# Two layers of a convolution and attention network: layer 1's merged, interleaved attention replaced by a plain loop over images, and the experts issued as a software pipeline over units of half an image

## The chip, the cores and the metric

The kernel runs on one core of one Trainium2 chip. The metric is the device time of one execution in microseconds (us); the median of three runs stands for a kernel. All arithmetic is in fp32.

## The reference

The input x has 8 images of 256 channels and 32 x 32 pixels (1024 tokens). Layer 0 is a convolution and attention block that the change does not touch. Layer 1 takes the tokens and computes, for each image:

```
t = t + attn(ln(t));   t = t + experts(ln(t))

attn(E): Q = E WQ^T;  K = E WK^T;  V = E WV^T
         W = Q K^T / 16                       # 1024 x 1024 an image, one head of 256
         e = exp(W - max over the whole row) * (1 where k <= q and W != 0, else 0)
         out = e / (sum e + 1e-9) @ V

experts(x): w = softmax(mean over the images of x @ Wr + br)     # a gate for each token and expert
            h = relu(bn(x W1[e] + b1));  h = relu(bn(h W2[e] + b2));  y = h Wo[e] + bo
            out = sum over the 8 experts of y * w                # every expert sees every token
```

`ln` is a layer norm over the 256 channels without weights. The maximum is over the whole row of W, also over masked places, so all 1024 columns of the logits are computed.

## The kernel before

Channels lie on the partitions in two groups of 128 (`KC`), the tokens of an image along the free dimension, in two halves of 512 (`HALF`). TensorE, VectorE (DVE), ScalarE (ACT), GpSimd (POOL) and SyncE (SP, which issues all DMAs) run side by side. Each fp32 matmul shows in the trace as two passes with a weight load each.

The program has three stages. Layer 0 writes each image to a spill buffer in DRAM, and all eight images are loaded back into `t[0..7]`. Layer 1's attention adds to `t`; `z[b]` is the normed image. The experts read `z` and add to `t`, which is stored.

**Layer 1 (L563 to L730).** At the start `wq` and `wk` are transposed and multiplied into one matrix `mT` (L572 to L591), so that the logits of an image are `(mT z) z^T`. For each image there are four kinds of work. `layer_norm` (L600) is a generator of three pieces: the two channel groups are summed on DVE into `ts` and their mean `mu` is one matmul with a constant matrix; the squares are summed with a thin matrix into `var`, four slices stacked on the partitions, so that the reciprocal runs over 256 elements; `r` is spread again with `sel4` into `rb`. `before1` (L638) norms an image and projects `y` and `v`. `after1` (L663) norms it a second time and adds it to `feat` for the gate. `logits(b, i)` (L670) computes the logits of 128 tokens in `s`, their maximum `nm`, the exponential `pr`, the causal mask on POOL, and the sum; `values(b, i)` (L702) transposes `pr` into `pT`, multiplies by `v` into `po`, scales by the reciprocal sum, transposes back into `tpo` and adds to `t`.

The main loop (L718) writes these in an interleaved order: the logits of tile i, then the values of the tile before, then a share of `before1` of the next image and of `after1` of the previous one.

**Buffers.** A tile pool hands out a fixed number of buffers for each tag. In PSUM `ps_s` has two of 1024 columns (`s`), `ps_t` two for transposes, `ps_m` two of 512 columns under the one tag `mm`: `mu`, `var`, `rb`, `pq`, `pv`, `po` and the gate's `lg` all take from it. In SBUF the tags `pr`, `pT`, `y` and `v` have two buffers each. The order of the instructions of an engine is set when the program is built, from the order written and from what is ready.

**Experts (L760 to L825).** For each expert e the three weight matrices are loaded (two buffers each) and the gate is spread to `wb`. For each image and half, a unit, three layers follow each other: h1 from z (L800, `w1s`), h2 from h1 (L800, `w2s`), then `pye` (L815, `wos`). Each layer is two output groups of two matmuls. ACT applies relu and the batch norm (L804), DVE adds the bias and multiplies by the gate (L819), POOL adds to `t` (L822). The last expert stores each image (L824). The inner order is

```
h1 = ...; layer(h1, w1s, z[b][:, :, hs], s1, o1)
h2 = ...; layer(h2, w2s, h1, s2, o2)
for g in range(KC):  # pye from h2, y, t += y
```

At the very end some tiny instructions (L830 on) check layer 0's sums; a general version of the program (L845 on) stands behind a branch that the inputs don't take.

Of the kernel before, what the change touches and what calls it, by code (L numbers as in the profile page):

```python
# [15 lines left out]
P = 128  # L16
# [62 lines left out]
def fast_body(  # L79
# [465 lines left out]


# [15 lines left out]

    with ExitStack() as l1:  # L563
        wpool = l1.enter_context(tc.tile_pool(name="w1", bufs=1))
        ps_s = l1.enter_context(tc.tile_pool(name="ps_s1", bufs=2, space=PSUM))
        ps_t = l1.enter_context(tc.tile_pool(name="ps_t1", bufs=2, space=PSUM))
        ps_m = l1.enter_context(tc.tile_pool(name="ps_m1", bufs=2, space=PSUM))


        mT = wpool.tile([P, KC, C], F32, name="mT")  # L570
        wv_s = wpool.tile([P, KC, C], F32, name="wv")
        nc.sync.dma_start(wv_s, wvT.rearrange("(k p) o -> p k o", p=P))  # L572
        with tc.tile_pool(name="wset", bufs=1) as wset:
            rows = []
            for nm_, src in (("wq", wqT), ("wk", wkT)):
                w_ = wset.tile([P, KC, C], F32, tag=nm_, name=nm_)
                nc.sync.dma_start(w_, src.rearrange("(k p) o -> p k o", p=P))
                r_ = wset.tile([P, KC, C], F32, tag=f"{nm_}r", name=f"{nm_}r")
                for e in range(KC):
                    tp = ps_t.tile([P, 4, P], F32, tag="tp", name="tpw")  # L580
                    for k in range(KC):
                        nc.tensor.transpose(tp[:, k, :], w_[:, k, e * P : (e + 1) * P], ident)
                    nc.vector.tensor_copy(r_[:, e, :], tp[:, :KC, :])
                rows.append(r_)
            for g in range(KC):
                pm_ = ps_m.tile([P, HALF], F32, tag="mm", name="pmT")
                for e in range(KC):
                    nc.tensor.matmul(
                        pm_[:, :C], rows[0][:, e, g * P : (g + 1) * P], rows[1][:, e, :], start=(e == 0), stop=(e == KC - 1)
                    )  # L590
                nc.scalar.activation(mT[:, g, :], pm_[:, :C], AF.Copy, scale=1.0 / math.sqrt(C))  # L591
        two = l1.enter_context(tc.tile_pool(name="two1", bufs=2))
        feat = wpool.tile([P, KC, N], F32, name="feat")
        sel4 = wpool.tile([P, 4, P], F32, name="sel4")
        nc.gpsimd.memset(sel4, 0.0)
        nc.gpsimd.affine_select(
            out=sel4, in_=sel4, compare_op=ALU.not_equal, fill=1.0, base=0, pattern=[[-32, 4], [0, P]], channel_multiplier=1
        )

        def layer_norm(b):  # L600

            tb, zb = t[b], z[b]
            for h in range(2):
                hs = slice(h * HALF, (h + 1) * HALF)
                ts = two.tile([P, HALF], F32, tag="ts", name="ts", bufs=1)
                nc.vector.tensor_add(ts, tb[:, 0, hs], tb[:, 1, hs])
                mu = ps_m.tile([P, HALF], F32, tag="mm", name="mu")
                nc.tensor.matmul(mu, mean_c, ts, start=True, stop=True)
                nc.vector.tensor_sub(
                    zb[:, :, hs], tb[:, :, hs], mu.rearrange("p (o n) -> p o n", o=1).to_broadcast([P, KC, HALF])  # L610
                )
            yield
            var = ps_m.tile([P, HALF], F32, tag="mm", name="var")
            for k in range(KC):
                sq = two.tile([P, N], F32, tag="sq", name="sq", bufs=1)
                nc.scalar.activation(sq, zb[:, k, :], AF.Square)
                for j in range(4):
                    nc.tensor.matmul(
                        var[32 * j : 32 * j + 32, :QC], mean_c[:, :32], sq[:, j * QC : (j + 1) * QC],
                        start=(k == 0), stop=(k == KC - 1),  # L620
                    )
            r = two.tile([P, QC], F32, tag="r", name="r", bufs=1)
            nc.scalar.activation(r, var[:, :QC], AF.Sqrt, bias=eps_ln)
            nc.vector.reciprocal(r, r)
            yield
            for h in range(2):
                hs = slice(h * HALF, (h + 1) * HALF)
                rb = ps_m.tile([P, HALF], F32, tag="mm", name="rb1")
                for i in range(2):
                    nc.tensor.matmul(rb[:, i * QC : (i + 1) * QC], sel4[:, 2 * h + i, :], r, start=True, stop=True)  # L630
                nc.vector.tensor_mul(
                    zb[:, :, hs], zb[:, :, hs], rb.rearrange("p (o n) -> p o n", o=1).to_broadcast([P, KC, HALF])
                )
            yield

        ys, vs = {}, {}

        def before1(b):  # L638
            yield from layer_norm(b)
            y = two.tile([P, KC, N], F32, tag="y", name="y")  # L640
            for g in range(KC):
                for h in range(2):
                    hs = slice(h * HALF, (h + 1) * HALF)
                    pq = ps_m.tile([P, HALF], F32, tag="mm", name="pq1")
                    for k in range(KC):
                        nc.tensor.matmul(
                            pq, mT[:, k, g * P : (g + 1) * P], z[b][:, k, hs], start=(k == 0), stop=(k == KC - 1)
                        )
                    nc.scalar.copy(y[:, g, hs], pq)
                yield  # L650
            v = two.tile([P, NT, C], F32, tag="v", name="v")
            for j in range(0, NT, 2):
                pv = ps_m.tile([P, 2, C], F32, tag="mm", name="pv")
                for i in range(2):
                    js = slice((j + i) * P, (j + i + 1) * P)
                    for k in range(KC):
                        nc.tensor.matmul(pv[:, i, :], z[b][:, k, js], wv_s[:, k, :], start=(k == 0), stop=(k == KC - 1))
                nc.scalar.copy(v[:, j : j + 2, :], pv)
                if j % 4 == 2:
                    yield  # L660
            ys[b], vs[b] = y, v

        def after1(b):  # L663
            yield from layer_norm(b)
            if b == 0:
                nc.gpsimd.tensor_copy(feat, z[b])
            else:
                nc.gpsimd.tensor_add(feat, feat, z[b])

        def logits(b, i):  # L670

            width = (i + 1) * P
            q0 = i * P
            s = ps_s.tile([P, N], F32, tag="s", name="s1")
            for h in range(2):
                hs = slice(h * HALF, (h + 1) * HALF)
                for k in range(KC):
                    nc.tensor.matmul(s[:, hs], ys[b][:, k, q0 : q0 + P], z[b][:, k, hs], start=(k == 0), stop=(k == KC - 1))  # L678

            nm = small.tile([P, 1], F32, tag="nm", name="nm1")  # L680
            nc.vector.tensor_reduce(nm, s, AX.X, ALU.max, negate=True)
            pr = two.tile([P, N], F32, tag="pr", name="pr1")
            nc.scalar.activation(pr[:, :width], s[:, :width], AF.Exp, bias=nm)
            nc.gpsimd.affine_select(
                out=pr[:, q0:width],
                in_=pr[:, q0:width],
                compare_op=ALU.is_ge,
                fill=0.0,
                base=0,
                pattern=[[-1, P]],  # L690
                channel_multiplier=1,
            )
            sm = small.tile([P, 1], F32, tag="sm", name="sm1")
            nc.vector.scalar_tensor_tensor(
                pr[:, :width], s[:, :width], 0.0, pr[:, :width], ALU.not_equal, ALU.mult, accum_out=sm
            )
            rs = small.tile([P, 1], F32, tag="rs", name="rs1")
            nc.vector.tensor_scalar_add(rs, sm, A_EPS)
            nc.vector.reciprocal(rs, rs)
            return pr, rs  # L700

        def values(b, i, pr, rs):  # L702

            pT = two.tile([P, NT, P], F32, tag="pT", name="pT1")
            transpose_rows(pr, (i + 1) * P, pT, 0, ps_t)
            po = ps_m.tile([P, HALF], F32, tag="mm", name="po1")
            for j in range(i + 1):
                nc.tensor.matmul(po[:, :C], pT[:, j, :], vs[b][:, j, :], start=(j == 0), stop=(j == i))
            ot = two.tile([P, C], F32, tag="ot", name="ot")
            nc.scalar.activation(ot, po[:, :C], AF.Copy, scale=rs)  # L710
# [9 lines left out]
        for b in range(B):  # L720
            prev = Stream(after1(b - 1), AFTER_PIECES) if b else None
            nxt = Stream(before1(b + 1), BEFORE_PIECES) if b + 1 < B else None
            for i in range(NT):
                cur = (b, i) + logits(b, i)
                if late is not None:
                    values(*late)
# [790 lines left out]
```

## Time and profile before

| what | us |
|---|---|
| median of three runs (3762.32 to 3765.38) | 3764.66 |
| the profiled execution | 3762.32 |
| its span | 3760.6 |
| layer 0 ends, all images in the spill buffer, about | 1679 |
| first norm of layer 1 starts (L606) | 1709.5 |
| last norm of layer 1 ends (L631) | 2318.2 |
| first expert matmul (L800) | 2343.8 |
| last store issued (L824) | 3752.8 |

| engine | busy us | share |
|---|---|---|
| PE (matmuls) | 3521.5 | 94% |
| PEld (weight loads) | 1599.2 | 43% |
| DVE | 1632.4 | 43% |
| ACT | 1412.6 | 38% |
| POOL | 389.3 | 10% |

PE is TensorE's matmuls and PEld its weight loads, which run beside them. The busy time of PE is modelled at the end of each matmul, so a short wait between two matmuls doesn't show in it; the starts of the weight loads show it. A line of the timeline gives start and duration in us, engine, line of the program, operation, tiles (output `<-` inputs), shape, count, and in brackets the idle time before it with what ended it. Durations of single instructions in the lists of groups are in ns.

### The profile page before, as it was taken

The page shows a single profiled execution, that of the slowest core. Times are in us where ns is not written, and L with a number is a line of the kernel's source. Part 1 is how long each engine was busy: PE and PEld are TensorE (multiplying, and loading weights), DVE is VectorE, ACT ScalarE, POOL GpSimd, SP SyncE. Part 2 cuts the span into 40 slices and gives each one's busy share as a digit, 9 for nine tenths or more (in the row PEclk, how much of TensorE's full clock was granted, in tenths as well). Part 3 has the DMA queues.
Part 4 walks back from the last instruction along what each step waited for, and adds up shares of the span by engine and source line. Part 5 has one row for each costly group of instructions (what it writes and reads, how often), then busy time and mean ns, then how long its engine had stood idle before and what let it go on. Part 6 is the DMA issues. An engine that isn't in the chain of part 4 may idle for free. (4 is left out here: it accounts for less than half of the span.)

```text
span 3760.6 us, 25274 instructions
## 1 busy us (share of the span) xinstructions
PE 3521.5 (94%) x9924; PEld 1599.2 (43%) x9924; DVE 1632.4 (43%) x1902; ACT 1412.6 (38%) x1850; POOL 389.3 (10%) x357
## 2 busy tenths in 40 slices
PE   7999999999999999737999997999999999999998
PEld 4334444343434343324655664444444444444443
DVE  3368585959595858653454443111111111111111
ACT  4354545455454544202344333222323222222222
POOL 1000000000000000000000101222222222222222
PEclk9999999999999999868999997999999999999999
DMA  1000000000000000011000000000000000000001
GB/s 63 0 0 0 23 0 23 1 23 0 23 0 23 0 12 0 12 64 45 1 1 1 1 1 17 0 9 0 9 1 9 0 9 0 9 0 9 0 34 57
DMA packets 16277, 45.05 MB, mean 12 GB/s; under 512 B 1350, under 2 KB 9494, under 8 KB 14102
## 3 DMA queue, kind: packets, MB, share of 16 engines
q1 hardware_dynamic: 16150, 43.36, 3.1%
q8 instruction: 80, 1.31, 0.1%
q14 instruction: 47, 0.39, 0.0%
HBM read 26.57 MB, written 16.78 MB: 12 GB/s over the span
## 5 line engine op out<-in xcount | busy, mean ns | idle before, releaser
L804 ACT ACTIVATE h<-pm,bn_o,bn_s 128x512 f32<-128x512 f32 x512 | 398.0, 777 | 967.1 <-PE pm L800 967.1
L819 DVE SCALAR_TENSOR_TENSOR y<-pye,vec,wb 128x512 f32<-128x512 f32 x256 | 192.1, 750 | 1219.3 <-PE pye L815 1218.0
L464 DVE SCALAR_TENSOR_TENSOR conv<-hpad,vec,conv 128x1024 f32<-128x1024 f32 x512 | 648.5, 1279 | 9.4
L397 PE MATMUL acc<-p,vT 128*128 128x512 f32 x1024 | 508.7, 629 | 62.9 <-ACT p L395 62.6
L800 PE MATMUL pm<-h,w2s 128*128 128x512 f32 x1024 | 494.5, 605 | 1.4
L815 PE MATMUL pye<-h,wos 128*128 128x512 f32 x1024 | 494.5, 605 | 1.4
L800 PE MATMUL pm<-z,w1s 128*128 128x512 f32 x1024 | 463.3, 595 | 0.0
L822 POOL TENSOR_TENSOR t<-t,y 128x512 f32<-128x512 f32 x256 | 323.6, 1264 | 1105.6 <-DVE y L819 1105.6
L397 PEld LDWEIGHTS acc<-p,vT 128*128 128x128 f32 x1024 | 192.2, 197 | 339.7 <-issue 173.1
L395 ACT ACTIVATE p<-s 128x1024 f32<-128x1024 f32 x256 | 254.9, 1021 | 216.3 <-PE s L393 215.4
L393 PE MATMUL s<-qk 32*128 32x512 f32 x1024 | 316.0, 632 | 0.0
L800 PEld LDWEIGHTS pm<-h,w2s 128*128 128x128 f32 x1024 | 184.0, 189 | 291.1 <-issue 153.6
L815 PEld LDWEIGHTS pye<-h,wos 128*128 128x128 f32 x1024 | 184.0, 189 | 291.1 <-issue 183.7
L800 PEld LDWEIGHTS pm<-z,w1s 128*128 128x128 f32 x1024 | 194.7, 191 | 249.2 <-issue 196.8
L330 PE MATMUL ph<-xn,piw 128*128 128x512 f32 x512 | 246.1, 613 | 18.0 <-ACT hpad L452 18.0
L678 PE MATMUL s<-z,y 128*128 128x512 f32 x512 | 247.2, 596 | 0.0
L393 PEld LDWEIGHTS s<-qk 32*128 32x128 f32 x1024 | 93.0, 184 | 180.3 <-issue 165.5
L560 POOL MEMSET ones<- 1x128 f32 x1 | 0.2, 194 | 1632.2 <-DVE conv L464 1632.2
L330 PEld LDWEIGHTS ph<-xn,piw 128*128 128x128 f32 x512 | 95.4, 194 | 157.3 <-issue 128.9
L480 PE MATMUL pz<-pow__122,hid 128*128 128x256 f32 x512 | 121.9, 389 | 42.9 <-DVE hid L473 42.9
L377 DVE SCALAR_TENSOR_TENSOR o<-vpad,pe_w,o 128x1024 f32<-128x1024 f32 x128 | 161.7, 1275 | 0.3
L452 ACT ACTIVATE hpad<-ph,pi_o 128x512 f32<-128x512 f32 x128 | 87.7, 688 | 173.6 <-PE ph L330 166.6
(190 smaller groups left out, 2943.6 us busy)
## 6 DMA issues: line engine op xcount, KB each, us to landing
t<-in_x_dram SPq DMA_DIRECT2D x8, 1024.0 KB, 5.0
sp<-t SPq DMA_DIRECT2D x8, 1024.0 KB, 3.9
t<-sp SPq DMA_DIRECT2D x8, 1024.0 KB, 9.9
out_dram<-t SPq DMA_DIRECT2D x8, 1024.0 KB, 4.0
w1s<-in_w_dram SPq DMA_DIRECT2D x8, 256.0 KB, 2.7
w2s<-in_w_dram SPq DMA_DIRECT2D x8, 256.0 KB, 2.8
wos<-in_wo_dram SPq DMA_DIRECT2D x8, 256.0 KB, 2.7
piw<-in_pi_wT_dram SPq DMA_DIRECT2D x1, 1024.0 KB, 8.7
```

The lines of the kernel that those rows point to most:

```text
L330: nc.tensor.matmul(ps, w[:, k, o0 : o0 + P], src[:, k, hs], start=(k == 0), stop=(k == KC - 1))
L377: nc.vector.scalar_tensor_tensor(d3, src, wk, d3, ALU.mult, ALU.add)
L393: nc.tensor.matmul(s[:, i, :], qk[kp, 1, m * P : (m + 1) * P], qk[kp, 0, cs], start=True, stop=True)
L395: nc.scalar.activation(p, s, AF.Exp)
L397: nc.tensor.matmul(acc[i], vT[:, m, g, i : i + 2, :], p[:, i, :], start=(m == 0), stop=(m == NT - 1))
L464: nc.vector.scalar_tensor_tensor(d3, src, wk, d3, ALU.mult, ALU.add)
L678: nc.tensor.matmul(s[:, hs], ys[b][:, k, q0 : q0 + P], z[b][:, k, hs], start=(k == 0), stop=(k == KC - 1))
L800: nc.tensor.matmul(pm, w_[:, k, g * P : (g + 1) * P], src[:, k, :], start=(k == 0), stop=(k == KC - 1))
L804: nc.scalar.activation(dst[:, g, :], pm, AF.Relu, bias=bi[:, c : c + 1], scale=sc[:, c : c + 1])
L815: nc.tensor.matmul(py, wos[:, k, g * P : (g + 1) * P], h2[:, k, :], start=(k == 0), stop=(k == KC - 1))
L819: nc.vector.scalar_tensor_tensor(y, py, col("bo", KC * e + g), wb[:, hs], ALU.add, ALU.mult)
L822: nc.gpsimd.tensor_add(t[b][:, g, hs], t[b][:, g, hs], y)
```

## The change

Layer 1 goes to a plain loop over the images. The merged matrix, `ts`, the thin `var`, `sel4` and the generators go. `wq`, `wk` and `wv` are used as loaded. One image after the other is normed, projected, attended and normed again. The norm takes the mean with two matmuls over t and sums the squares with two matmuls over 512 columns, so that `r` and its reciprocal are 128 x 512. The squares are taken on POOL. Queries go in blocks of 256 (`QC`): two tiles of logits, with `pr` scaled by the reciprocal sum on POOL ahead of the transposes, then one `po` with the channels on the partitions, which is added to `t` directly. The pool `one1` gives one buffer each to `sq`, `r`, `q`, `k`, `v` and `pT`.

In the experts a list of units is kept, and step n issues h1 of unit n, h2 of unit n - 1 and `pye` of unit n - 2; `h1` and `h2` have three buffers. Two more steps at the end finish the last units.

```diff
+    def layer_norm(b, work, ps_m):
+        for h in range(2):
+            hs = slice(h * HALF, (h + 1) * HALF)
+            mu = ps_m.tile([P, HALF], F32, tag="mm", name="mu")
+            for k in range(KC):
+                nc.tensor.matmul(mu, mean_c, t[b][:, k, hs], start=(k == 0), stop=(k == KC - 1))
+            sq = work.tile([P, KC, HALF], F32, tag="sq", name="sq")
+            for k in range(KC):
+                nc.vector.tensor_sub(z[b][:, k, hs], t[b][:, k, hs], mu)
+                nc.gpsimd.tensor_mul(sq[:, k, :], z[b][:, k, hs], z[b][:, k, hs])
+            var = ps_m.tile([P, HALF], F32, tag="mm", name="var")
+            for k in range(KC):
+                nc.tensor.matmul(var, mean_c, sq[:, k, :], start=(k == 0), stop=(k == KC - 1))
+            r = work.tile([P, HALF], F32, tag="r", name="r")
+            nc.scalar.activation(r, var, AF.Sqrt, bias=eps_ln)
+            nc.vector.reciprocal(r, r)
+            for k in range(KC):
+                nc.vector.tensor_mul(z[b][:, k, hs], z[b][:, k, hs], r)
...
+        one = l1.enter_context(tc.tile_pool(name="one1", bufs=1))
...
-        mT = wpool.tile([P, KC, C], F32, name="mT")
...
+        def causal_attention(b):
+            layer_norm(b, one, ps_m)
+            q = one.tile([P, KC, N], F32, tag="q", name="q")
+            kk = one.tile([P, KC, N], F32, tag="k", name="kk")
+            for g in range(KC):
+                for h in range(2):
...
+                    for w_, dst, sc in ((wq_s, q, 1.0 / math.sqrt(C)), (wk_s, kk, 1.0)):
+                        pq = ps_m.tile([P, HALF], F32, tag="mm", name="pq1")
...
+                        nc.scalar.activation(dst[:, g, hs], pq, AF.Copy, scale=sc)
+            v = one.tile([P, NT, C], F32, tag="v", name="v")
...
+                nc.vector.tensor_copy(v[:, j : j + 2, :], pv)
+            for qc in range(N // QC):
+                nq = QC // P
+                pT = one.tile([P, NT, QC], F32, tag="pT", name="pT1")
+                for qt in range(nq):
...
+                    s = ps_s.tile([P, N], F32, tag="s", name="s1")
...
+                    nc.vector.tensor_reduce(nm, s, AX.X, ALU.max, negate=True)
+                    pr = two.tile([P, N], F32, tag="pr", name="pr1")
+                    nc.scalar.activation(pr[:, :width], s[:, :width], AF.Exp, bias=nm)
+                    nc.gpsimd.affine_select(out=pr[:, q0:width], in_=pr[:, q0:width],
...
+                    nc.vector.scalar_tensor_tensor(
+                        pr[:, :width], s[:, :width], 0.0, pr[:, :width], ALU.not_equal, ALU.mult, accum_out=sm
+                    )
+                    nc.vector.tensor_scalar_add(rs, sm, A_EPS)
+                    nc.vector.reciprocal(rs, rs)
+                    nc.gpsimd.tensor_scalar(pr[:, :width], pr[:, :width], rs, 1.0, ALU.mult, ALU.mult)
+                    transpose_rows(pr, width, pT, qt * P, ps_t)
+                po = ps_m.tile([P, KC, QC], F32, tag="mm", name="po1")
+                nj = (qc + 1) * nq
+                for g in range(KC):
+                    for j in range(nj):
+                        c0 = max(0, j * P - qc * QC)
+                        nc.tensor.matmul(
+                            po[:, g, c0:], v[:, j, g * P : (g + 1) * P], pT[:, j, c0:], start=(j == 0), stop=(j == nj - 1)
+                        )
+                tb = t[b][:, :, qc * QC : (qc + 1) * QC]
+                nc.vector.tensor_add(tb, tb, po)
+
+        for b in range(B):
+            causal_attention(b)
+            layer_norm(b, one, ps_m)
             if b == 0:
                 nc.gpsimd.tensor_copy(feat, z[b])
             else:
                 nc.gpsimd.tensor_add(feat, feat, z[b])
...
+        def advance(n):
+            if n <= len(units):
+                e, b, h, w1s, w2s, wos, wb = units[n - 1]
+                hidden[n - 1] = layer("h1", w1s, z[b][:, :, h * HALF : (h + 1) * HALF], s1, o1, e)
+            if 0 <= n - 2 < len(units):
+                e, b, h, w1s, w2s, wos, wb = units[n - 2]
+                hidden[n - 2] = layer("h2", w2s, hidden[n - 2], s2, o2, e)
+            if 0 <= n - 3:
+                e, b, h, w1s, w2s, wos, wb = units[n - 3]
+                h2 = hidden.pop(n - 3)
...
+                if e == NE - 1 and h == 1:
+                    nc.sync.dma_start(ov[b], t[b])
...
             for b in range(B):
                 for h in range(2):
+                    units.append((e, b, h, w1s, w2s, wos, wb))
+                    advance(len(units))
+        for i in range(2):
+            advance(len(units) + 1 + i)
```

The new `layer` is the old one with the tile taken inside it and three buffers, and the part of `advance` left out is the old loop over `pye`, `y` and the sum into `t`.

## The prediction

> **What bounds the kernel now.** I read the busy shares first, then the same by stage, then the waits and the order of instructions inside a stage.
>
> ```profile
> PE 3521.5 (94%) x9924; PEld 1599.2 (43%) x9924; DVE 1632.4 (43%) x1902; ACT 1412.6 (38%) x1850; POOL 389.3 (10%) x357
> ```
>
> ```profile
> 1750.00:2300.00 550.00, 548.90 (x2211) 335.98 (x2210) 267.23 (x474) 220.76 (x348) 47.14 (x70) 1.00 0.00 1
> 2300.00:2343.00 43.00, 24.93 (x90) 16.53 (x89) 13.93 (x33) 9.07 (x23) 6.48 (x3) 0.58 0.11 34
> ...
> 2350.00:3750.00 1400.00, 1397.19 (x3092) 564.68 (x3090) 191.34 (x255) 405.10 (x525) 321.30 (x255) 1.00 0.03 9
> ```
>
> The second fence is the table by stretches; its lines give length, busy time of PE, PEld, DVE, ACT, POOL, then the granted clock. TensorE fills both stages that the change touches. In layer 1 (1750 to 2300) it is busy 548.9 of 550 us for eight images: 68.7 us per image, at full clock. In the experts it seems equally full, but ends of matmuls are modelled, so I look at when weights are loaded:
>
> ```profile
> 2905.57 0.19 PEld L800 LDWEIGHTS pm<-z,w1s 128*128 128x128 f32 x1 [0.24 <-DVE y L819]
> ...
> 2909.01 0.19 PEld L800 LDWEIGHTS pm<-h,w2s 128*128 128x128 f32 x1 [0.24 <-ACT h L804]
> ...
> 2910.47 0.30 PEld L800 LDWEIGHTS pm<-h,w2s 128*128 128x128 f32 x2 [0.84 <-ACT h L804]
> ...
> 2912.72 0.19 PEld L815 LDWEIGHTS pye<-h,wos 128*128 128x128 f32 x1 [0.24 <-issue]
> ...
> 2914.18 0.30 PEld L815 LDWEIGHTS pye<-h,wos 128*128 128x128 f32 x2 [0.84 <-ACT h L804]
> ...
> 2916.43 0.19 PEld L800 LDWEIGHTS pm<-z,w1s 128*128 128x128 f32 x1 [0.24 <-DVE y L819]
> ```
>
> Layer w1s, which reads z, takes 3.44 us (2905.57 to 2909.01) for 8 passes (each fp32 matmul is two): 0.43 us a pass. Layers w2s and wos take 3.71: their second k tile waits for the ACT relu of the layer just before. That is 0.27 us lost twice per unit of 10.86 us. Over 128 units the waits list has
>
> ```profile
> PEld pm L800 <- ACT h L804: 137.5, 254, 0.8
> PEld pye L815 <- ACT h L804: 107.4, 128, 0.8
> ```
>
> most of which is the ordinary distance between loads; only 2 x 0.27 us per unit is lost.
>
> One more reading decides what the new layer 1 can overlap. The program is put in order per engine when it is built, not as written: at 52.12 a logits matmul (L393) runs between transposes (L363) that stand before it. But tiles of one pool tag are handed out in the order written:
>
> ```profile
> 9.73 1.04 ACT L306 ACTIVATE xn<-t 128x1024 f32<-128x1024 f32 x1
> ...
> 17.30 3.57 PE L227 MATMUL wv<-vec,qkvw 128*128 128x1 f32 x16
> ...
> 29.33 1.93 PE L310 MATMUL ms<-xn,mean_c 128*32 128x256 f32 x16
> ```
>
> The squares for ms are ready at 10.77 and TensorE is idle until 16.2, yet ms runs at 29.33, after all the wv tiles, its predecessors in tag mm. The same at 1717: image 1's ts is summed at 1716.66, TensorE has gaps until 1727, but mu comes at 1744, in its written place.
>
> [...]at 2343.81 the first expert passes stand 0.85 us apart, from 2348.19 on 0.43; the window 2300 to 2343 has a granted clock of 0.58. [...]layer 1 has 15 of 1283 ns for Sqrt and 15 for Exp in the groups of 1600 to 2300, run ahead of their operand, and the new code needs as many (one to Sqrt, one to Exp an image). For the new POOL scaling of pr no row exists; see below.
>
> **Experts.** The new order puts, between a layer and its reader, at least one other layer of another unit, 3.4 us of TensorE work against a relu of 0.78. ACT (4 x 0.78 us), DVE (2 x 0.75) and POOL (2 x 1.26) have room in 10.3 us, h1 and h2 get a third buffer. On SP, a weight buffer comes free two units later (21 us) for the loads of the expert after next, which have 174 us; the store of an image is issued at its second half, two units after it was, again with 21 us of other units behind it. So 2 x 0.27 x 128 = 69, say **70 us gained**; bounds 0 (a new wait) and 75. The last image's store (3752.8 to the span's end) stays uncovered as it is.
>
> **Layer 1, TensorE work per image.** Two norms of 8 matmuls: 16 x 0.86 = 13.8 (before: ones over ts, thin var, rb). q and k: 16 x 0.86 = 13.8 (merged matrix: 6.9). v: 32 passes of 256 columns at 0.21 = 6.9. Logits 32 x 0.86 = 27.5. Transposes 36 x 0.11 = 3.9 (the ot ones go). po: 32 x 0.43 + 8 x 0.22 = 15.5. Sum 81 against 68.7. Costed at nothing: the q and k copies (8 of 0.59 on ACT in place of 4) and the v copies, now on DVE (4 of 0.69), each under 1.72 us of its next matmuls; ot's scaling, gone from ACT; the sums into t, 4 in place of 8. That is the floor; the order now leaves holes, since norms, projections and po share tag mm, and q, k, v, pT, sq, r have one buffer. So image b+1's norm can't enter before b's second norm, and b's second norm not before its last po. Per image:
>
> Norm pair, from the end of the last po. First half: mu 1.7, subtract 0.69, squares on POOL 2 x 1.26 (row L822), var after them, Sqrt 0.69 (row L452, same form), reciprocal 3.35 (row L414, 128x512), two multiplies of 0.69 (row L422): with hand-overs 13 us. Each further half must wait for r, then Sqrt, reciprocal, multiplies: 0.7 + 3.35 + 1.4 = 5.5, plus 0.7 for a subtract in between, plus the squares, which wait for sq. I get 8.8 for the second, 6.2 for the third, and 7.6 for the fourth, where the feat sum (4.5 us, row L668) sits ahead of the squares on POOL. **36 us**; bounds 30 (reciprocal chain alone) and 42 (half clock, squares slowed).
>
> Projections: the first q and k group hides in the norm; 6 x 1.72 + 6.9 = 17.2, plus 2 for a cold start: **19**; bounds 17 and 23.
>
> Attention: after the last pass of logits i come max 1.22, Exp 0.38 to 1.13, mask 0.29, product 0.29 to 1.22, sum and reciprocal 0.4, POOL scaling, then transposes. The scaling I take at 0.2 + 0.9 ns an element, 0.3 to 1.1 us, from the POOL COPY of 2048 elements (1889 ns)[...]. With two s buffers, logits i+1 and i+2 cover this chain, so TensorE is full for six tiles. By priority the third po (4.7) goes ahead of the end of the eighth logits: these end 40 us after the start. Then nothing covers the last chain: 6 us, transposes and copy 1.3, po 6.5, of which a part at half clock, +2: **55 us**; bounds 49 and 65.
>
> Sum 36 + 19 + 55 = 110 us per image against 68.7.
>
> **Front and end.** The norm of image 0 needs only t[0], the first of eight 1 MB loads issued from 1679 on; at 437 GB/s it lands near 1682. Now wq and wk are transposed and multiplied first (1703 to 1709.8) and the norm starts at 1709.5. So 27 us are won there. Its 22 us end near 1704, when the projection weights, last in the queue, have landed (wk at 1703 now). New end of the last norm: 1682 + 22 + 8 x 74 + 7 x 36 + 22 = 2570, against 2318 now (last multiply 2316.93 + 1.22). **+252 us.** Gate and expert set-up after it are unchanged.
>
> **Sum.** +252 - 70 = +182 on the profiled execution of 3762.3 (span 3760.6 and 1.7 around it). The median of the three runs is 3764.7, so 3947; I say 3945.
>
> **Rivals.** *Overlap after all* (the other side): if the builder does let image b+1's norm run in b's attention, layer 1 is bound by TensorE at 81 us an image. The end is 1690 + 8 p for p us an image (110 gives 2570), so 81 gives 2338: +20 - 70 = -50, 3715. It is faster from p below 87 (1690 + 8 x 87 = 2388). For it: logits are moved ahead. Against: ms and mu above never were. 0.10, of which 0.02 within 0.2% of no change. *Serial tiles*: if transposes i stay ahead of logits i+1, each tile pays 3.4 plus the whole chain: 8 x 3.4 + 8 x 4.9 + 4 + 15.5 + 3 = 89 us, p = 144, end 2842: +524 - 70, 4219[...]. Against: the move at 52.12. 0.10. *Expert gain missing* (a wait on another buffer replaces it): 4017. 0.05. My forecast: 0.75.
>
> **Range.** p from 96 to 130 gives -112 and +160 about 3945. I take 3840 to 4100, which takes in the missing expert gain and leaves out the overlap and the serial case: 0.2. Differences below 0.2% (7.5 us) can't be told from none by a measurement of this kernel. Faster 0.08, within 0.2% 0.02, slower 0.90.
>
> **What would show it.** Expert units of 10.3 us with relu waits gone; last norm's multiply near 2570; 36 us a pair between images with TensorE mostly idle and a clock near 0.5; before each image's last transposes an idle 6 us. Wrong: mu of image b+1 inside attention b (first rival), or 9 us and more from logits to logits (second).

## The result, and the profile after

| kernel | median us | lowest to highest | ratio to before, 95% interval |
|---|---|---|---|
| before, in the same session | 3763.49 | 3759.99 to 3765.38 | |
| after | 3958.36 | 3955.81 to 3959.01 | 1.0518 (1.0499 to 1.0536) |

The change costs 195 us. The profiled execution after took 3958.95 us, its span is 3957.2, 196.6 more than before; all that follows is read against that. From the profile's page, the busy times of the kernel after:

```profile
PE 3600.7 (91%) x9780; PEld 1652.5 (42%) x9780; DVE 1734.9 (44%) x1946; ACT 1349.2 (34%) x1754; POOL 512.1 (13%) x483
```

and its table by stretches (length, busy time of PE, PEld, DVE, ACT, POOL, granted clock, DMA share, GB/s), for layer 1, the end of layer 1 and the experts:

```profile
1702.00:2535.00 833.00, 691.38 (x2054) 364.34 (x2054) 361.26 (x508) 158.89 (x255) 156.78 (x184) 0.90 0.00 1
2535.00:2600.00 65.00, 45.26 (x173) 30.09 (x172) 27.80 (x45) 13.32 (x25) 17.27 (x16) 0.80 0.00 0
2600.00:3940.00 1340.00, 1338.32 (x3114) 591.64 (x3115) 192.42 (x266) 408.54 (x536) 319.25 (x252) 0.99 0.03 10
```

The experts still look full; layer 1 no longer does. TensorE had hardly a gap there before (1.1 of 550 us); now it is idle for 142 of 833 us, and its clock is granted only 0.90. Yet 691 busy us, in a layer that took 609 in all (1709.5 to 2318.2), also mean more work, or slower work. The rest of this section separates these.

**Experts.** The timeline of weight loads after, at the start of each layer of one unit (start, duration, then in brackets the idle time and what ended it):

```profile
2998.37 0.19 PEld L724 LDWEIGHTS pm<-z,w1s 128*128 128x128 f32 x1 [0.24 <-DVE y L749]
...
3001.80 0.19 PEld L724 LDWEIGHTS pm<-h,w2s 128*128 128x128 f32 x1 [0.24 <-ACT h L728]
...
3005.24 0.19 PEld L745 LDWEIGHTS pye<-h,wos 128*128 128x128 f32 x1 [0.24 <-issue]
...
3008.67 0.19 PEld L724 LDWEIGHTS pm<-z,w1s 128*128 128x128 f32 x1 [0.24 <-DVE y L749]
```

All three layers now take 3.43 to 3.44 us, the unit 10.30 in place of 10.86, and the wait of 0.84 us on the relu is gone. From the first expert matmul (2611.4) to the last output's y (3946.9) are 1335.5 us, against 1406.8 before (2343.8 to 3750.6): 71 us won.

**Layer 1.** The first expert matmul comes at 2611.4 in place of 2343.8: 267.6 us lost. 267.6 - 71.3 is 196.3, the whole difference. The stretches of one steady image, from the end of the last `po` of the image before: the pair of norms, the projections, the attention:

```profile
2113.90:2160.20 46.30, 28.79 (x44) 9.58 (x43) 26.22 (x21) 3.94 (x6) 13.85 (x9) 0.71 0.00 1
2160.20:2177.20 17.00, 17.00 (x57) 10.64 (x56) 2.07 (x3) 3.58 (x6) 0.00 (x0) 1.00 0.00 0
2177.20:2226.80 49.60, 47.58 (x179) 28.85 (x179) 20.61 (x44) 13.75 (x22) 8.30 (x16) 1.00 0.00 0
```

This image takes 112.9 us, the mean of the last six is 112.6. For before the same table, from one sum of features to the next:

```profile
2022.30:2094.80 72.50, 72.50 (x293) 44.22 (x293) 35.73 (x63) 29.58 (x46) 6.81 (x9) 1.00 0.00 1
```

So a steady image took 72.5 us, not the 68.7 that I had got by dividing 550 us by eight: that stretch holds some 7.6 images. The forecast's sum did not use the figure, since it counts from the first norm to the last, but the comparison of floors did. TensorE is now idle 17.5 us in the pair and 2.0 in the attention, together 19.5. It is busy 93.4; at full clock its work would be about 81.4 (the prediction's sum, unrounded). So, as an estimate, some 12 us of its busy time are lost to half-clock passes, and 8.9 us (81.4 - 72.5) are added work. 19.5 + 12 + 8.9 = 40.4, which is 112.9 - 72.5. The largest part is idle time, the next half clock, and added work the least.

### The profile page after: what moved, and what is told of

It reads as the page before. It is cut to its first block, busy times and chain, and to the rows that moved or that the text cites. A ratio compares the mean times of both kernels' runs of the same rounds, so it can differ in the third digit from the quotient of the medians.

```text
span 3957.2 us, 25092 instructions
## 1 busy us (share of the span) xinstructions
PE 3600.7 (91%) x9780; PEld 1652.5 (42%) x9780; DVE 1734.9 (44%) x1946; ACT 1349.2 (34%) x1754; POOL 512.1 (13%) x483
## 3 DMA queue, kind: packets, MB, share of 16 engines
q8 instruction: 79, 1.29, 0.1%
## 4 chain that ended last, share of the span: by engine, by line
PE 71%; DVE 19%; ACT 4%; issue 2%; POOL 2%; DMA 1%; ACTq 0%; SPq 0%; DVEq 0%; POOLq 0%
PE pm L724 22%; PE pye L745 11%; DVE conv L464 9%; PE acc L397 7%; PE s L393 3%; PE ph L330 3%; PE s L630 3%; PE po L661 3%; DVE o L377 3%; PE pq L607 3%; PE pz L480 3%; PE pq L330 2%; PE var L574 2%; DVE r L577 1%; PE pv L617 1%
## 5 line engine op out<-in xcount | busy, mean ns | idle before, releaser
L724 PE MATMUL pm<-h,w2s 128*128 128x512 f32 x1024 | 460.3, 592 | 0.0
L745 PE MATMUL pye<-h,wos 128*128 128x512 f32 x1024 | 460.2, 592 | 0.0
L750 POOL TENSOR_TENSOR t<-t,y 128x512 f32<-128x512 f32 x256 | 324.3, 1267 | 1031.3 <-DVE y L749 1031.3
L724 PEld LDWEIGHTS pm<-h,w2s 128*128 128x128 f32 x1024 | 194.6, 190 | 244.9 <-issue 213.6
L745 PEld LDWEIGHTS pye<-h,wos 128*128 128x128 f32 x1024 | 194.6, 190 | 244.9 <-issue 244.9
L630 PE MATMUL s<-kk,q 128*128 128x512 f32 x512 | 236.4, 597 | 10.4 <-DVE pr L648 5.6
L574 PE MATMUL var<-sq,mean_c 128*128 128x512 f32 x128 | 107.6, 946 | 123.8 <-POOL sq L571 123.8
```

The source lines that it names most:

```text
L630: nc.tensor.matmul(s[:, hs], q[:, k, q0 : q0 + P], kk[:, k, hs], start=(k == 0), stop=(k == KC - 1))
L724: nc.tensor.matmul(pm, w_[:, k, g * P : (g + 1) * P], src[:, k, :], start=(k == 0), stop=(k == KC - 1))
L745: nc.tensor.matmul(py, wos[:, k, g * P : (g + 1) * P], h2[:, k, :], start=(k == 0), stop=(k == KC - 1))
L750: nc.gpsimd.tensor_add(t[b][:, g, hs], t[b][:, g, hs], y)
```

## The experiments

Each row is the median of four runs; an image's time is from `po` end to `po` end (for e1 from one sum of features to the next), read from the timelines of images 2 to 6. The pair runs from the first mean of the second norm to the last product of the next image's norm.

| run | us | an image | pair of norms |
|---|---|---|---|
| after | 3958.4 | 112.1 to 112.9 | 45.3 to 46.4 |
| e1_layer1_before | 3691.8 | 72.5 to 72.7 | beside attention |
| e2_experts_before | 4031.9 | 112.1 to 112.9 | 45.3 to 46.4 |
| e3_squares_act | 3910.9 | 104.8 to 107.6 | 37.3 to 39.3 |
| e4_norms_written_early | 3863.4 | 98.7 to 99.0 | beside attention |
| e5_no_feat_sum | 3940.8 | 110.8, then 112.5 to 112.8 | 42.6, then 44.2 to 44.3 |
| e8_norm_before | 3923.4 | 107.4 to 109.0 | 37.5 to 38.7 |
| e9_merged_qk | 3945.5 | 109.1 to 109.2 | 47.8 to 48.0 |
| e10_norm_before_early | 3821.8 | 95.3 to 95.9 | beside attention |
| e11_merged_norm | 3889.6 | 100.5 to 102.1 | 37.5 to 38.6 |
| e12_merged_no_feat | 3910.3 | 106.3, then 105.8 to 105.9 | 43.9 to 44.1 |
| e13_one_group_twice | 3981.8 | 113.6, then 116.1 to 116.3 | 45.3, then 47.9 to 48.1 |
| e6_two_buffers | 3959.3 | 112.1 to 113.9 | 45.3 to 46.8 |

### The two halves of the change alone

Layer 1 from before with the pipeline, and layer 1 from after with the old expert loop; nothing else is edited.

> Layer 1 as before, the experts as a pipeline. Theory (the change is two independent terms, the experts gain about 71 us of a 10.86 us unit that becomes 10.30 us, and layer 1 loses about 268): 3763 - 71 = 3692 us, the first expert matmul still at about 2344 us, no wait at the start of L728's readers. Rival (the pipeline pays only because layer 1 hands over differently, or because the whole clock history is different): within 20 us of 3763.

> Layer 1 as after, the experts layer by layer as before. Theory of two independent terms: 3958 + 71 = 4029 us, with the 0.8 us waits of TensorE back at the first matmul of the second and third layer. Rival as in the run above: within 20 us of 3958.

3691.8 and 4031.9 us against 3692 and 4029. The pipeline gains 72.5 us with the old layer 1 (3764.3 in that session) and 73.6 with the new one: the two parts touch each other by no more than about 1 us. Layer 1 as before, and the experts in the run with them as before (table by stretches for the first, timeline of loads for the second):

```profile
1750.00:2300.00 550.00, 548.89 (x2208) 335.31 (x2207) 268.20 (x474) 220.99 (x348) 47.13 (x70) 1.00 0.00 1
```

```profile
3201.54 0.19 PEld L752 LDWEIGHTS pye<-h,wos 128*128 128x128 f32 x1 [0.24 <-issue]
3202.57 0.30 PEld L752 LDWEIGHTS pye<-h,wos 128*128 128x128 f32 x2 [0.84 <-ACT h L741]
```

The wait is back with the old loop. Layer 1 as before with the pipeline is also the best kernel of this study: 0.9806 of before (0.979 to 0.9823).

### Form or order: what in layer 1 costs

Three things that the change alters in layer 1 can carry the loss: the form of the norm, the query-key matrix, and the order (a plain loop in place of streams written between each other). Each of the two forms of before was put back alone, then both; the order stayed plain, and so did the blocks of 256 queries and the single buffers.

```
# e8: the generator layer_norm(b) of before without its yields,
#     with sel4 and pool `two`, called in place of layer_norm(b, one, ps_m)
# e9
-  for w_, dst, sc in ((wq_s, q, 1.0 / math.sqrt(C)), (wk_s, kk, 1.0)):
+  for w_, dst, sc in ((mT, q, 1.0),):      # mT built as before
-  s[:, hs], q[:, k, q0 : q0 + P], kk[:, k, hs], ...
+  s[:, hs], q[:, k, q0 : q0 + P], z[b][:, k, hs], ...
# e11: both
```

> The change with the norm written as before (one sum of the two channel groups, squares of 1024 on ScalarE, one packed square root and a 256-wide reciprocal of 1.74 us for the image), still in plain order. Theory (a bare norm costs the sum of its steps): 0.7 + 0.9 + 1.2 + 1.2 + 2 x 1.1 + 1 + 0.5 + 1.7 + 0.9 + 2 x 1.2 + 1.5 of hand-overs = 14 us, the pair 26 to 30 in place of 45.6: 3958 - 8 x 17.5 = 3818 us (3800 to 3840). Rival (the half-image chains overlap so well that the form does not matter, only the order does): 3930 us or more.

> The change with the merged query-key matrix back (one projection in place of two, logits against z), norms and order as in the change. Theory: eight matmuls less per image, 8 x 0.86 = 6.9 us x 8 = 55 us won, and 25 to 27 us lost again at the start, where the matrix is built ahead of image 0: 3958 - 55 + 26 = 3929 us. Rival (the second projection is hidden behind other waits): 3970 us or more.

> The change with both forms of before (merged query-key matrix and the norm of before), still in plain order: against the run with layer 1 as before (3692 us) only the order is left. Theory (the order is most of the loss in layer 1, the forms little): the two forms alone gave 35 and 13 us, together 45 to 80 us: 3878 to 3913 us, so that the order alone is worth 186 to 221 of the 267 us. Rival (the forms bring their loss back once both are there): 3850 us or less.

The norm's form is worth 35 us, where I expected 140; the matrix 13, where I expected 29; both 69. In e9 the matrix costs what I forecast at the start (the first norm begins 29.6 us after the first load is issued, in place of 5.3), but an image gains only 3.4 of the 6.9 us taken off TensorE; "Steps of 3.41 us" returns to this. From e11 to layer 1 as before **198 us** remain (3889.6 - 3691.8), three quarters of the loss. One steady image of e11 by stretches:

```profile
2092.40:2194.24 101.84, 80.59 (x286) 46.29 (x285) 41.98 (x62) 21.29 (x32) 12.75 (x17) 0.85 0.00 1
```

TensorE is idle for 21.3 us of it and its mean clock is 0.85, though it has no more work than before: the same matmuls, without the transposes of `ot`. So the 198 us are waits and half clock, which is what a changed order would bring, and the order is the main difference left. The values in blocks of 256, their scaling on POOL and the single buffers differ too, and no run puts them back alone: how much of the 198 us is the order by itself is not shown.

My sum for the bare norm of before (14 us) was too small. Its timeline shows one reason, which returns below: `ts`, a sum of two operands in SBUF that takes 0.68 us in the kernel before (L606), took 3.50 beside the sum of features on POOL.

```profile
2006.91 4.50 POOL L692 TENSOR_TENSOR feat<-feat,z 128x2048 f32<-128x2048 f32 x1 [25.74 <-DVE z L612]
2007.31 1.22 DVE L592 TENSOR_TENSOR z<-t,mu 128x1024 f32<-128x1024 f32 x1 [0.49 <-PE mu L591]
2008.45 3.50 DVE L589 TENSOR_TENSOR ts<-t 128x512 f32<-128x512 f32 x1
```

### Is it the place in the queue?

The same instructions and buffers as in the change, but the first norm of image b+1 and the second of image b-1 written between projections and attention of b; once with the new norm, once with that of before.

```
-            layer_norm(b, one, ps_m)                # head of causal_attention
 ... projections of b ...
+            fill(b)     # layer_norm(b + 1), then layer_norm(b - 1) and its feat
             for qc in range(N // QC):
```

> The change with the same tiles, buffers and instructions, but the first norm of image b+1 and the second of image b-1 are written between the projections and the attention of image b. Theory (the norms lie bare because their matmuls stand in TensorE's queue behind the last product of the image before; what else they need is free): the norms' two or three first half-chains run beside the first logits and the last beside the second round, an image goes from 112.7 to 85 to 97 us, the kernel to 3958 - 8 x 22 = 3782 us (3720 to 3840). Rival (the attention's own work on VectorE and ScalarE, or the one buffer each for squares and deviations, lets nothing run beside it): an image stays at 105 or above, 3900 us or more.

> The norm as before, written between the projections and the attention as in the run with early norms. Theory (in that run the norms' work on VectorE, four halves of 6.3 us = 25 us a pair, stands ahead of the softmax's maxima and stretches the attention by 28 us): the form of before puts 16 us a pair on VectorE, the attention is stretched by 15 to 19 us, an image takes 86 to 90 us in place of 98.9, and the kernel 3863 - 8 x 11 = 3775 us (3755 to 3800). Rival (it is the waits of TensorE for squares and means inside the logits that stretch it, whatever VectorE does): 3840 us or more.

Moving them is worth 95 us with the new norm and 102 with the old one (3923.4 - 3821.8), so the place in the queue is a cause; but both expectations were too good, by 81 and 47 us. The table by stretches of the attention of one image with the early new norms shows why:

```profile
2008.20:2086.40 78.20, 66.43 (x213) 35.80 (x213) 45.62 (x64) 17.69 (x27) 22.08 (x25) 0.96 0.00 0
```

The attention alone has TensorE busy 47.6 of 49.6 us. There is hardly room in it: what the norms put on TensorE is added in full (66.4 - 47.6 = 18.8 us, where the prediction priced them at 13.8 at full clock; here the clock is 0.96), and only the waits of their chain can be covered. Of these a part stays, since the softmax's own work on VectorE now stands behind the norm's. VectorE's timeline in the same run:

```profile
2015.47 1.88 PE L630 MATMUL s<-kk,q 128*128 128x512 f32 x4
...
2016.27 3.35 DVE L577 RECIPROCAL r<-r 128x512 f32<-128x512 f32 x1
...
2020.08 2.13 DVE L579 TENSOR_TENSOR z<-z,r 128x512 f32<-128x512 f32 x2
...
2022.13 1.21 DVE L635 TENSOR_REDUCE nm<-s 128x1 f32<-128x1024 f32 x1
```

The first logits are complete at 2017.35; their maximum waits behind the norm's reciprocal and products until 2022.13. The same stage with the old norm:

```profile
2082.30:2157.30 75.00, 63.62 (x238) 37.12 (x237) 35.19 (x58) 21.36 (x30) 13.11 (x17) 0.93 0.00 1
```

VectorE is busy 10.4 us less, TensorE 2.8, and the image went from 98.9 to 95.5. That is near what TensorE does less, so 10 us off VectorE bought little. But 3.4 us is also one of the steps that are described below, so the two shares are not separated by this run.

### What is in the 46 us of the pair

Three suspects: POOL (its squares, and the sum of features ahead of one of them), the single buffers for squares and deviations, and TensorE's half clock.

```
# e3
-  nc.gpsimd.tensor_mul(sq[:, k, :], z[b][:, k, hs], z[b][:, k, hs])
+  nc.scalar.activation(sq[:, k, :], z[b][:, k, hs], AF.Square)
# e5
-  else:
-      nc.gpsimd.tensor_add(feat, feat, z[b])
# e6
-  sq = work.tile(..., name="sq");          r = work.tile(..., name="r")
+  sq = work.tile(..., name="sq", bufs=2);  r = work.tile(..., name="r", bufs=2)
```

> The change with one line altered: the norm's squares on ScalarE in place of POOL. Theory (the pair of norms takes 46 us and not 36 because the squares share POOL with the sum of features and hold up VectorE's two-operand products beside them): two half-image norms lose some 4 to 5 us behind the sum, and all four some 0.5 to 1 us of slow products and subtractions; the pair goes to 36 to 39 us and the kernel to 3958 - 8 x 8 = 3895 us (3875 to 3915). Rival (the pair is long because TensorE's passes are at half clock there, 0.85 to 1.04 us each, and because of the reciprocal's 3.35 us): no more than 2 us a pair, 3940 to 3958 us.

> The change without the sums of the second norms into feat for images 1 to 7 (left out: the mean of the norms over the images, the gate sees image 0 alone); squares stay on POOL. Theory (most of what the squares lost on POOL is the 4.5 us sum standing ahead of the third half's second square): seven images lose 4.5 to 5 us each and the tail one more: 3958 - 8 x 4.7 = 3920 us; the product with r stays at 0.99 us. Rival (the loss is the products and squares slowing each other, not the queue): 3950 us or more.

> The change with two buffers each for the squares and the deviations of the norm. Theory (a norm's length is its chain over VectorE, POOL and TensorE, and the place in the queue decides that it lies bare; the buffers have long been free when they are asked for): within 8 us of 3958. Rival (one buffer holds up the next half's squares and square root): the pair of norms 3 to 6 us shorter, 3910 to 3935 us.

Second buffers for squares and deviations change nothing (3959.3). The squares on ScalarE gave 47 us, with a pair of 37 to 39 as expected. Groups of instructions (busy us, mean ns of one, idle before), first after, then with the squares on ScalarE:

```profile
L574 PE MATMUL var<-sq,mean_c 128*128 128x512 f32 x112 | 94.6, 948 | 110.7 <-POOL sq L571 110.7
L579 DVE TENSOR_TENSOR z<-z,r 128x512 f32<-128x512 f32 x56 | 53.6, 999 | 0.7
```

```profile
L574 PE MATMUL var<-sq,mean_c 128*128 128x512 f32 x112 | 83.4, 864 | 75.8 <-ACT sq L571 75.8
L579 DVE TENSOR_TENSOR z<-z,r 128x512 f32<-128x512 f32 x56 | 35.9, 683 | 0.2
```

VectorE's product `z<-z,r` has both operands in SBUF. With POOL's squares its mean is 999 ns, without them 683. In the kernel after, a pair of products took 2.12 us where POOL's square ran beside it (2125.82, square from 2125.98) and 1.29 at the end of the same pair of norms, with no square beside it (2158.89). The 3.50 us of `ts` above fit to that: it ends half a us after POOL's sum. The subtraction `z<-t,mu`, which reads one operand from PSUM, took 0.68 us where the sum of features began beside it (2136.35) and 0.66 in the mean of the kernel after. These are the times; what makes the products longer is not shown.

The sum of features (e5 leaves it out, so that the gate sees image 0 alone) was the miss. In the kernel after it does hold up the third half's second square (timeline of the same image as above):

```profile
2136.35 0.68 DVE L570 TENSOR_TENSOR z<-t,mu 128x512 f32<-128x512 f32 x1
2136.51 4.50 POOL L673 TENSOR_TENSOR feat<-feat,z 128x2048 f32<-128x2048 f32 x1 [0.63 <-DVE z L579]
...
2140.97 1.04 POOL L571 TENSOR_TENSOR sq<-z 128x512 f32<-128x512 f32 x1
2142.06 2.08 PE L574 MATMUL var<-sq,mean_c 128*128 128x512 f32 x2 [2.34 <-POOL sq L571]
```

Without it the square comes 3.86 us sooner after its predecessor, yet from image 3 on an image takes 112.5 to 112.8 us, as before. The 17.6 us that the kernel gained all the same lie elsewhere: its gate need not wait for the last image, so that the first expert matmul follows the last norm after 12.5 us in place of 25.5, and in the profiled execution layer 0 ended 5.1 us sooner. Where the 3.86 us went is seen by setting the same passes beside each other, after and then without the sum:

```profile
2117.53 2.12 PE L574 MATMUL var<-sq,mean_c 128*128 128x512 f32 x4 [1.90 <-POOL sq L571]
2119.49 1.88 PE L567 MATMUL mu<-t,mean_c 128*128 128x512 f32 x4
...
2154.47 1.97 PE L607 MATMUL pq<-z,wq 128*128 128x512 f32 x4
```

```profile
2110.86 3.06 PE L574 MATMUL var<-sq,mean_c 128*128 128x512 f32 x4 [1.90 <-POOL sq L571]
2113.71 2.69 PE L567 MATMUL mu<-t,mean_c 128*128 128x512 f32 x4
...
2145.63 3.62 PE L607 MATMUL pq<-z,wq 128*128 128x512 f32 x4
```

The same passes, four in each line, take 0.94, 0.81 and 1.65 us more: TensorE's clock fell earlier in the pair (4.7 us after the last `po`, against 10.0) and came back later (after 42.2 us, against 40.7). 3.4 of the 3.86 us are spent in half-clock passes.

### Steps of 3.41 us

When does the clock change? The stretches of the pair after, cut where it does (the figure after POOL's is the granted clock):

```profile
2122.00:2123.90 1.90, 0.63 (x2) 0.30 (x2) 1.90 (x2) 0.00 (x0) 1.04 (x1) 1.00 0.00 0
2123.90:2130.70 6.80, 5.58 (x8) 1.80 (x6) 4.25 (x5) 0.69 (x1) 1.42 (x1) 0.50 0.00 0
2130.70:2134.15 3.45, 0.46 (x1) 0.00 (x0) 3.45 (x2) 0.00 (x0) 0.00 (x0) 0.99 0.00 0
2134.15:2154.60 20.45, 11.63 (x13) 3.77 (x14) 9.41 (x9) 0.69 (x1) 9.36 (x5) 0.50 0.00 1
2154.60:2160.00 5.40, 4.71 (x12) 1.94 (x11) 4.46 (x3) 1.88 (x3) 0.00 (x0) 1.00 0.00 2
```

The changes lie 6.80, 3.45 and 20.45 us apart, 30.70 together: 2, 1 and 6 times 3.41 (30.70 / 9), to the 0.05 us of these cuts. In the last of the three TensorE is busy 11.6 of 20.5 us, at a granted clock of 0.50 throughout. An image of 112.6 us is 33.0 such steps; one with the merged matrix (109.2), which takes 6.9 us off TensorE, is 32.0. So I suspected that the time of an image is pulled to whole steps: an image that comes earlier finds the full clock later, and pays what it had won. Two runs were made for this, one that takes work out of TensorE and POOL, one that adds 1.72 us to the projections, where TensorE has no gap and full clock.

```
# e12: edits of e5 and e9 together
# e13
-  for k in range(KC):
+  for k in [*range(KC)] * (2 if g + h == 2 and w_ is wk_s else 1):   # in the q/k projections
```

> The merged query-key matrix back, and the sums of the second norms into feat left out for images 1 to 7 (the gate then sees image 0 alone). Each of these alone left the steady image at a whole number of steps of 3.41 us[...]: 112.6 (33 steps) without the sum, 109.2 (32 steps) with the merged matrix. Theory (the time of an image is pulled to such steps, so that a gain smaller than a step is lost in half-clock passes, and the two together show what each hid): an image takes 102.4 or 105.8 us, the kernel 3893 or 3917 us. Rival (the sum costs nothing and the matrix 3.4 us, whatever the reason): 109.2 us an image, 3928 us.

> The change with one projection group of each image computed twice into the same tile: 4 passes, 1.72 us of TensorE more per image, in a stage in which TensorE has no gap and full clock. Theory of steps (as in the run above): a steady image stays at 112.6 us or goes up a whole step to 116.0; the kernel takes 3958 to 3964 or 3978 to 3985 us. Rival (times add): 114.3 us an image, 3972 us.

3910.3 us at 105.8 an image (31.0 steps), and 3981.8 at 116.1 (34.0). Adding times would have given 109.2 an image and 3928, and 114.3 and 3972. Two images of the second run by stretches:

```profile
2120.10:2236.20 116.10, 96.72 (x283) 50.36 (x281) 48.92 (x68) 21.26 (x34) 22.11 (x25) 0.87 0.00 1
2236.20:2352.30 116.10, 96.73 (x283) 50.42 (x282) 48.92 (x68) 21.25 (x34) 22.10 (x25) 0.87 0.00 0
```

1.72 us of work became 3.4, and images repeat to 0.01 us of TensorE's busy time. The sum of features, free with two projections, was worth 3.4 us an image (109.2 to 105.8) with the merged matrix: the same edit, on the two sides of a step. The kernels with early norms lie on whole steps too (98.9 us is 29.0, 95.5 is 28.0). The images with squares on ScalarE (104.8 to 107.6) and those with the norm of before in plain order (107.4 to 109.0, 100.5 to 102.1) do not; there the pattern of half and full clock changes from one image to the next. What decides between the two is not shown.

## Why the prediction held, point by point

- **The sum.** Forecast 3945, measured 3958.4: +182 against +195. Experts -70 was -71; layer 1 +252 was +268 (last norm's product ends at 2585.9, forecast 2570).
- **Experts.** The reading held in every part: 2 x 0.27 us a unit, relu waits gone, no new wait on h1, h2 or a weight buffer; e1 and e2 confirm it with 72.5 and 73.6 us, under either layer 1.
- **Added TensorE work.** The floor of 81 was right where it can be read: the attention's part, 46.9 us, stands against 47.6 busy. What it was compared with was wrong, 68.7 in place of 72.5: the added work is 8.9 us an image, not 12.
- **Norm pair: 36 forecast, 45.6 the mean of seven, outside my bound of 42.** This is the step that failed. Halves of images 1 to 2: 14.2, 8.5, 14.4 and 9.2 us, against 13, 8.8, 6.2 and 7.6. The third half carries it: I had put the sum of features ahead of the fourth half's squares and priced it there at 1.4 us (7.6 - 6.2); it stands ahead of the third half's second square, inside the chain. After image 0, where a copy of 1.9 us stands in its place, the third half took 11.8 us. What e3 removed (the squares' place on POOL, and VectorE's longer products beside them, 999 ns in place of 683) was 7 us of the pair, with what followed from it on the clock; the two are not separated. Multiplies that I took at 0.69 us from a row without POOL beside it were 1.00. The half clock that I allowed only in the upper bound was there in 27 of 46 us (6.80 + 20.45 at 0.50). The sign that I had named was off too: TensorE is busy 28.8 of 46.3 us there, not mostly idle, and its clock 0.71, not near 0.5.
- **Attention: 55 forecast, 49.7 measured, and projections 19 against 17.** The 2 us for a cold start of the projections were my estimate; these 17.0 us have a granted clock of 1.00. I expected an idle 6 us ahead of the last transposes. The timeline of TensorE at the end of an image after:

```profile
1986.72 1.02 PE L630 MATMUL s<-kk,q 128*128 128x512 f32 x2
1987.58 4.92 PE L661 MATMUL po<-pT,v 128*128 128x256 f32 x24
1992.34 0.93 PE L163 MATMUL tp<-ident,pr 128*128 128x128 f32 x7
1993.77 1.06 PE L163 MATMUL tp<-ident,pr 128*128 128x128 f32 x8 [0.49 <-ACT pT L164]
1995.07 6.75 PE L661 MATMUL po<-pT,v 128*128 128x256 f32 x32 [0.24 <-ACT pT L164]
2001.66 1.88 PE L567 MATMUL mu<-t,mean_c 128*128 128x512 f32 x4
```

The third `po` runs after the eighth logits, not ahead of them, and with the seventh transposes it covers the last tile's softmax: the idle time is 0.49 + 0.24 us. With that the stage has no half-clock part either (granted clock 1.00 in its 49.60 us). The last line is the mean of the same image's second norm, at once after the last `po`: the place in the queue that I had argued for.

- **Two errors that cancelled.** Against the formula 1682 + 22 + 8 x 74 + 7 x 36 + 22: start +3.4 us (the first mean began at 1685.4), first norm +4.2 (26.2 us), projections and attention 8 x -7.3 = -58, pairs 7 x 9.6 = +67, last norm -0.7; together +16, by which the last product was late. With only one of the two misses the forecast would have been off by some 50 to 75 us. The image (110 against 112.6) was right only as a sum, by luck.
- **Table loads.** I had as many for the new code as for the old. Layer 1 has 9 for Sqrt and 8 for Exp, against 16 and 15 before (I had counted up to 2300: 15 and 15), each 1.28 us in both kernels. The sum had no term for them.
- **The rivals.** *Serial tiles* and the *missing expert gain* did not come. *Overlap after all* did not come, and e4 shows that its price was wrong as well: with the norms really in the attention an image takes 98.9 us, not the floor of 81, and the kernel 3863, not 3715. It would not have crossed the deciding 87. I had treated TensorE's floor as reachable. In e4 TensorE is idle for some 12 us of each image and partly at half clock (0.96 in the mean of the 78.20 us above), while maxima of the softmax wait on VectorE behind the norm. The streams of before reach 72.5 us with TensorE hardly ever idle.

## What to carry to other kernels

Look where a chain that waits on several engines is written: among the matmuls of other work, or between them. Here, between them, a pair of norms lay bare for 46.3 us, with TensorE idle for 17.5 of them and its clock at 0.71. The forms of norm and projection gave 69 of 267 us, and 198 remain, in which the order is the main difference; moving the norms alone brought back 95 to 102. Before pricing an overlap, look how full the covering stage already is on the shared engine: the attention, busy 47.6 of 49.6 us, hid waits of the norms, but their 18.8 us on TensorE were added in full. And where a loop has a stage in which TensorE partly waits, test a change of a few us with a second one before calling it worthless: here a square that came 3.86 us sooner did not shorten an image, and 1.72 us of added work cost 3.4.

## What the runs showed of the hardware that was not expected

- In the kernel after, the granted clock of a pair of norms went between 1.00 and 0.50 at distances of 6.80, 3.45 and 20.45 us, multiples of 3.41. The time of an image came to rest on whole multiples of the same 3.41 us in most of the kernels with such stages (31, 32, 33 and 34 of them in e12, e9, after and e13, 29 and 28 in e4 and e10: 105.8, 109.2, 112.6, 116.1, 98.9 and 95.5 us); in e3, e8 and e11 it did not. 1.72 us of added matmuls cost 3.4, and a 4.5 us POOL sum taken out of the chain gained an image nothing until another edit moved the loop to another step.
- Two of VectorE's instructions with both operands in SBUF took longer beside POOL's: `ts` 3.50 us in place of 0.68 beside the 4.50 us sum (e8), a pair of products 2.12 in place of 1.29 beside a square (after). The square was longer beside them as well, 1.42 us in place of 1.04.
- POOL's square of a tile (the same operand twice) took 1.04 us alone for 512 elements, against 1.27 for the experts' sums of two operands (L750), and its scaling by a value per partition 0.37 us for 128 and 1.13 for 1024.
